# A list scheduler's overlap constants: a graph network kernel planned with less overlap between successive instructions on ScalarE, VectorE and GpSimd

## The chip, the cores and the metric

The kernel runs on one core of one Trainium2 chip. The core has five queues that run asynchronously: TensorE (PE, matrix products), ScalarE (ACT), VectorE (DVE), GpSimd (POOL) and SyncE (SP, which issues the DMAs here). Each works through its own instructions in order. The metric is the device time in microseconds (us); less is better. Where the text says "put", it means an ACT copy that empties a PSUM bank into SBUF.

## The reference

Inputs are 128 graphs of 128 nodes with 256 features, `x`, and 128 adjacency matrices, `adj`. Two layers with layer norm ahead of each are computed:

```python
# layer 0: three gated graph steps (GRU)
h = jnp.maximum(_layernorm(x, axis=-1), 0.0)
for i in range(3):
    m = jnp.einsum('bnd,de->bne', h, weight[i])
    aggr = jnp.einsum('bst,bsd->btd', A, m)          # A = (adj != 0)
    h = _gru_cell(aggr, h, w_ih, w_hh, b_ih, b_hh)
x = x + h
# layer 1: graph attention
h = jnp.maximum(_layernorm(x, axis=-1), 0.0)
Wh = h @ W;  s = Wh.sum(axis=-1)
e = jax.nn.leaky_relu(s[:, :, None] + s[:, None, :], negative_slope=0.2)
alpha = jax.nn.softmax(jnp.where(adj == 0, -jnp.inf, e), axis=-1)
x = x + alpha @ Wh
```

The GRU cell has gates r, z and n: `r` and `z` are sigmoids of sums over both inputs, `n = tanh(i_n + r * h_n)`, and `h = (1 - z) * n + z * h`.

## The kernel before

**Tiling.** The 128 graphs are taken in 32 groups of 4, so that a tile is 128 partitions by 512 columns (4 graphs of 128 nodes). A step of one group is a *turn*; there are 96 turns, and the list `turns` interleaves three groups: step 0 of group g, step 1 of group g-1, step 2 of group g-2. A turn is given 18.15 us (`SLOT`) in the plan, and it takes about 21.6 us, since other products of PE run between.

**A turn.** The state `hT` (features by nodes) is split into three bf16 parts on ACT and POOL (`turned_parts`, L609 to L616, or for rows `parts_of`, L591 and L594), turned by DMA transposes on SP (L580), and multiplied with the adjacency on PE (`edge_sums`, L634, bf16). ACT copies the sums to `aT` (L637). `node_sums` (L677 to L681) makes sums of blocks of `hT` (on POOL, `hs`) and of `aT` (on DVE, `gs`), since the weight products use a scheme with seven products in place of eight. `products` then issues the seven products for each kind, "rz" and "n", into PSUM banks `x_*`, `y_*` and `q_*`. In the first two steps of a group these are the matmuls of L708, in the last step (rows by features, `gru_rows`) those of L722.

**The put.** The bank `y_rz` is used twice in succession: product six is accumulated, `put` (L754) copies it to `t2_rz`, and product seven is accumulated on top and copied to `t3_rz`. PE runs product six of "n" between; product seven of "rz" may not start before the put of "rz" is done. DVE adds `q_rz` (L764). Gates follow on ACT (tanh, L810, L828, L834; L860 and L878 for rows) and DVE (L814 to L825, L837 to L843).

**Attention.** After step 2 of a group: layer norm (`normed`: DVE L514 and L519, POOL L523 and L524, DVE L526, ACT L530), scores, softmax (ACT exp, L1066), turned by DMA (`turned_halves_of`, ACT L1174 and L1178), PE L663 and L1099. `turned_halves` (ACT L570 and L574) turns rows by DMA likewise.

**What sets the order.** All operations are first recorded by `plan.op(engine, ns, fn, reads, writes, ...)` with a cost in ns; `Plan.run` is a list scheduler that simulates the five engines with these costs and emits the instructions in the order found. Nothing of its clock reaches the chip: only the order within each queue, and the buffers chosen along the way. The constants of the class describe the engines:

- `OVER`: by how much the next operation of an engine may start before the one ahead has ended. This is what the change edits.
- `LAG`, `SIGNAL`: what a wait across engines costs; `FLIP`: what PE loses from bf16 back to f32 matmuls; `HANDOFF`: for the port shared by DVE and POOL.

The three lines that use them are

```python
t = max(clock[e] + (self.FLIP if thin and e == "PE" and not nodes[i][8] else 0), at[i])
...
done = t + n[1]
clock[e] = done - self.OVER[e]
```

Of the operations of an engine that could start no later than the earliest possible start, the one with the smallest `rank` is taken. A rank is the latest time at which an operation must start so that the products behind it meet their due times; an operation that feeds PE's products has a further 7 us (`MARGIN`). PE's products (`due=plan.cursor`) form a chain in a fixed order; its other matmuls (edge sums, attention, transposes) are placed between by rank.

Of the kernel before, what the change touches and what calls it, by code (L numbers as in the profile page):

```python
# [41 lines left out]
class Plan:  # L42
# [5 lines left out]


    LAG = {"PE": 163, "ACT": 0, "DVE": 0, "POOL": 0, "SP": 3600}  # L50
    OVER = {"PE": 0, "ACT": 103, "DVE": 84, "POOL": 42, "SP": 0}
    FLIP, HANDOFF = 56, 120
    SIGNAL = {"PE": 53, "ACT": 36, "DVE": 36, "POOL": 78, "SP": 28}

# [62 lines left out]
    def run(self):  # L117
# [54 lines left out]
        while len(order) < len(nodes):  # L172
# [26 lines left out]
            done = t + n[1]  # L199
            clock[e] = done - self.OVER[e]  # L200
            if n[6]:
# [1013 lines left out]
```

## Time and profile before

Times of three runs: 2112.46, 2112.8 and 2113.26 us, median 2112.8. The profiled execution took 2112.71 us, its span (first to last instruction) was 2110.9 us at full TensorE clock.

| engine | busy, us | share of the span | instructions |
|---|---|---|---|
| PE (matmul) | 2084.3 | 99% | 10624 |
| PEld (weight load) | 1658.4 | 79% | 10624 |
| DVE | 1680.2 | 80% | 3626 |
| ACT | 1594.6 | 76% | 2977 |
| POOL | 921.5 | 44% | 881 |

Busy is the time in which the engine had at least one instruction running, so overlapped time counts once. A row of the waits names the waiting instruction, what it waited for, and the total in us, the number of times and the longest. A row of the timeline gives start and duration in us, the engine, the line, what is written and read, and in brackets the idle time ahead of it and what ended that.

### The profile page before, as it was taken

How to read it: one execution, taken by the hardware profiler on the slowest of the kernel's cores; microseconds unless marked ns; L12 is line 12 of the kernel's file. 1: busy time of each engine (PE TensorE's matmuls, PEld its weight loads, DVE VectorE, ACT ScalarE, POOL GpSimd, SP SyncE). 2: the span in 40 equal slices, each digit the busy share in tenths (PEclk: the TensorE clock that was granted, in tenths of full speed). 3: DMA queues.
4: the chain of work that ended last, by engine and by line, in shares of the span. 5: the costliest groups of instructions: out<-in, count | busy, mean ns of one | idle time of the engine just before them, and what ended most of it. 6: DMA issues, size and time to landing. Idle time of an engine off the chain costs nothing.

```text
span 2110.9 us, 30632 instructions
## 1 busy us (share of the span) xinstructions
PE 2084.3 (99%) x10624; PEld 1658.4 (79%) x10624; DVE 1680.2 (80%) x3626; ACT 1594.6 (76%) x2977; POOL 921.5 (44%) x881
## 2 busy tenths in 40 slices
PE   9999999999999999999999999999999999999998
PEld 7887887777877778877778777788777888788776
DVE  6678888788877887878878778887787778778777
ACT  5577877777777777777777777777778877867676
POOL 5445554334444444443355434444443444345230
PEclk9999999999999999999999999999999999999999
DMA  4322222332233223232223332232322323123321
GB/s 120 70 59 48 56 57 65 71 60 55 68 68 80 55 54 72 68 73 70 55 61 63 73 74 57 55 75 63 78 60 55 70 64 78 36 55 66 77 74 36
DMA packets 365147, 137.01 MB, mean 65 GB/s; under 512 B 296384, under 2 KB 364736, under 8 KB 364992
## 3 DMA queue, kind: packets, MB, share of 16 engines
q1 hardware_dynamic: 364992, 135.05, 29.1%
q8 instruction: 84, 1.38, 0.3%
q14 instruction: 71, 0.58, 0.1%
HBM read 45.36 MB, written 16.78 MB: 29 GB/s over the span
## 4 chain that ended last, share of the span: by engine, by line
PE 79%; ACT 10%; DVE 7%; issue 2%; DMA 0%; POOL 0%; SPq 0%; DVEq 0%; ACTq 0%; POOLq 0%
PE y_rz L708 14%; PE x_rz L708 10%; PE q_rz L708 8%; PE y_n L708 7%; PE y_rz L722 5%; PE misc L1099 5%; PE y_n L722 5%; PE misc L634 5%; PE x_n L708 4%; PE q_n L708 4%; PE q_rz L722 3%; PE x_n L722 3%; PE x_rz L722 3%; PE q_n L722 3%; ACT h L530 2%
## 5 line engine op out<-in xcount | busy, mean ns | idle before, releaser
L677 POOL TENSOR_TENSOR hs<-hT 128x512 f32<-128x512 f32 x96 | 129.5, 1350 | 304.5 <-PE y_n L722 238.9
L591 POOL TENSOR_TENSOR r<-rows 128x512 f32<-128x512 f32 x126 | 143.0, 1154 | 225.3 <-ACT rows L574 160.9
L764 DVE TENSOR_TENSOR t_rz<-t_rz,q_rz 128x512 f32<-128x512 f32 x192 | 130.8, 681 | 132.5 <-ACT t_rz L754 123.4
L754 ACT COPY t_rz<-y_rz 128x512 f32<-128x512 f32 x192 | 112.2, 584 | 146.4 <-PE y_rz L708 136.1
L708 PE MATMUL y_rz<-hs,s_hh 128*128 128x256 f32 x768 | 200.0, 383 | 1.0 <-ACT t_rz L754 0.9
L708 PE MATMUL y_rz<-gs,s_x 128*128 128x256 f32 x768 | 197.1, 379 | 0.0
L708 PEld LDWEIGHTS y_rz<-hs,s_hh 128*128 128x128 f32 x768 | 142.8, 190 | 27.1 <-ACT t_rz L754 9.2
L708 PEld LDWEIGHTS y_rz<-gs,s_x 128*128 128x128 f32 x768 | 145.9, 190 | 19.8
L594 POOL TENSOR_TENSOR p<-r 128x512 bf16<-128x512 f32 x126 | 156.9, 1264 | 0.0
L681 POOL TENSOR_TENSOR hs<-hT,hs 128x256 f32<-128x256 f32 x96 | 75.3, 785 | 177.1 <-PE q_n L722 160.7
L834 ACT ACTIVATE u<-u,bias_i 128x512 f32<-128x512 f32 x128 | 92.8, 725 | 74.0 <-DVE u L825 73.8
L764 DVE TENSOR_TENSOR t_n<-t_n,q_n 128x512 f32<-128x512 f32 x192 | 130.3, 678 | 19.9 <-ACT t_n L754 17.8
L898 POOL TENSOR_TENSOR x<-x,u 128x512 f32<-128x512 f32 x60 | 77.6, 1294 | 147.9 <-ACT u L878 62.8
L708 PE MATMUL x_rz<-hT,s_hh 128*128 128x256 f32 x512 | 131.4, 379 | 0.0
L708 PE MATMUL x_rz<-aT,s_x 128*128 128x256 f32 x512 | 131.4, 379 | 0.0
L840 DVE SCALAR_TENSOR_TENSOR d<-rz,d 128x512 f32<-128x512 f32 x128 | 117.6, 920 | 0.9
L637 ACT COPY aT<-misc 128x512 f32<-128x512 f32 x190 | 102.8, 581 | 18.1 <-PE misc L634 17.9
L616 POOL TENSOR_TENSOR pl<-d,pl 128x512 bf16<-128x512 f32 x64 | 75.7, 1183 | 89.9 <-ACT pl L614 89.8
L708 PE MATMUL y_n<-gs,s_x 128*128 128x256 f32 x384 | 114.3, 379 | 0.0
L708 PE MATMUL y_n<-hs,s_hh 128*128 128x256 f32 x384 | 114.3, 379 | 0.0
L837 DVE TENSOR_TENSOR d<-hT,u 128x512 f32<-128x512 f32 x128 | 107.3, 839 | 8.5 <-ACT u L834 6.3
L611 POOL TENSOR_TENSOR d<-hT,pl 128x512 f32<-128x512 f32 x64 | 85.6, 1339 | 63.7 <-ACT pl L609 59.0
(286 smaller groups left out, 6297.9 us busy)
## 6 DMA issues: line engine op xcount, KB each, us to landing
rows<-in_x_dram SPq DMA_DIRECT2D x32, 512.0 KB, 4.2
x<-in_x_dram SPq DMA_DIRECT2D x32, 512.0 KB, 3.9
out_dram<-x SPq DMA_DIRECT2D x31, 512.0 KB, 2.9
at<-in_adj_dram SPq DMA_DIRECT2D x32, 256.0 KB, 3.2
plT<-pl SPq DMA_TRANSPOSE x186, 3.3
peT<-pe SPq DMA_TRANSPOSE x60, 3.1
e<-in_L_gnn_weight_dram SPq DMA_DIRECT2D x3, 256.0 KB, 3.7
rz<-in_L_gnn_w_ih_dram SPq DMA_DIRECT2D x2, 384.0 KB, 4.3
```

The source lines that it names most:

```text
L591: op("POOL", 1042, lambda part=part: nc.gpsimd.tensor_tensor(ap(r1)[:, part], ap(rows)[:, part], top(rows)[:, part], OP.subtract), [(rows, ...
L594: op("POOL", 1042, lambda part=part: nc.gpsimd.tensor_tensor(ap(p3)[:, part], ap(r1)[:, part], top(r1)[:, part], OP.subtract), [(r1, n, n ...
L634: nc.tensor.matmul(flat(ps)[:, b * N:(b + 1) * N], part(i, b, k), ap(a)[:, b, :], start=(i == 0), stop=(i == 2))
L637: op("ACT", 590, lambda k=k, ps=ps: nc.scalar.copy(ap(dst)[:, k, :], flat(ps)), [ps], [(dst, 2 * k, 2 * k + 2)])
L677: op(eng, cost, lambda: sub(ap(w)[:, 0:2, :], blocks()[:, 1::2, :], blocks()[:, 0:2, :], OP.subtract), [t], [(w, 0, 2)], two=True)
L708: nc.tensor.matmul(ap(bank)[:, half, :], ap(w)[:, i - 1, gate, :], source(i, t, sums), start=(first and c == 0 and m == 0), stop=False, sk ...
L722: op("PE", 645, lambda c=c, w=w, t=t, sums=sums: nc.tensor.matmul(flat(bank)[:, c * P:(c + 3) * P], source(i, t, sums)[:, m * N:(m + 1) * ...
L754: op("ACT", 590, lambda: nc.scalar.copy(ap(t), ap(y)), [y], [t], mark=mark)
L764: op("DVE", 690, lambda: nc.vector.tensor_tensor(ap(t), ap(t), ap(q), OP.add), [q], [t])
L837: op("DVE", 690, lambda j=j, d=d, cols=cols: nc.vector.tensor_tensor(ap(d), ap(hT)[:, j, :], ap(u)[:, cols], OP.subtract), [(hT, lo, hi), ...
L840: op("DVE", 690, lambda d=d, cols=cols: nc.vector.scalar_tensor_tensor(ap(d), ap(rz)[:, 1, cols], 1.0, ap(d), op0=OP.add, op1=OP.mult), [( ...
L1099: nc.tensor.matmul(ap(ps)[:, b, :], ap(uT)[:, k, (m + b) * N:(m + b + 1) * N], ap(w1)[:, k, :], start=(k == 0), stop=(k == KD - 1))
```

## The change

Three of the five constants in `OVER` are lowered: ACT from 103 to 50, DVE from 84 to 40, and POOL from 42 to -100, which is a gap of 100 ns in place of an overlap. `PE` and `SP` stay at 0. Costs, due times, ranks' rules and the program's operations are untouched.

```diff
     LAG = {"PE": 163, "ACT": 0, "DVE": 0, "POOL": 0, "SP": 3600}
-    OVER = {"PE": 0, "ACT": 103, "DVE": 84, "POOL": 42, "SP": 0}
+    OVER = {"PE": 0, "ACT": 50, "DVE": 40, "POOL": -100, "SP": 0}
     FLIP, HANDOFF = 56, 120
```

## The prediction

> **What bounds the kernel now.** I read the page's first part, then TensorE's (PE's) own waits, then the timelines around the wait that recurs.
>
> ```profile
> PE 2084.3 (99%) x10624; PEld 1658.4 (79%) x10624; DVE 1680.2 (80%) x3626; ACT 1594.6 (76%) x2977; POOL 921.5 (44%) x881
> ```
>
> PE is idle for 2110.9 - 2084.3 = 26.6 us. Everything else on the page hides behind it, so the change can act only through these 26.6 us, through new idle time on PE, and through how PE's instructions overlap. The list of PE's waits says what the idle time is:
>
> ```profile
> PE y_rz L722 <- ACT t_rz L754: 14.1, 19, 1.3
> PE q_n L1160 <- DVE eT L1158: 1.4, 1, 1.4
> PE y_rz L708 <- ACT t_rz L754: 0.9, 2, 0.7
> ```
>
> 15.0 us are waits for one kind of ScalarE (ACT) copy, the "put" of line 754, which empties the PSUM bank y_rz before PE may accumulate into it again. PE's timeline places the others: 5.0 us in the first 30 us (seven waits, 0.16 to 1.27 us), 2.6 us from 2048 us on (five waits), and 3.8 us after PE's last matmul. The 19 waits of L722 lie between 325 and 1556 us, spaced by 64.8 us from 453 us on (453.26, 518.68, 583.45, ... 1555.67), nearly all 0.68 to 0.77 us long: the plan is periodic with three turns, and it has one stall in each period. After 1556 us the same plan has none. One such period, ACT and PE:
>
> ```profile
> 1032.24 0.72 ACT L834 ACTIVATE u<-u,bias_i 128x512 f32<-128x512 f32 x1 [1.40 <-DVE u L825]
> 1032.87 0.57 ACT L668 COPY uT<-misc 128x512 f32<-128x512 f32 x1
> 1033.34 2.08 ACT L530 ACTIVATE h<-x,nm,rs 128x256 f32<-128x256 f32 x4
> 1035.40 1.04 ACT L570 COPY pl<-hT 128x1024 uint16<-128x1024 uint16 x1
> 1036.35 0.58 ACT L754 COPY t_rz<-y_rz 128x512 f32<-128x512 f32 x1
> ```
>
> ```profile
> 1034.18 0.81 PE L722 MATMUL y_rz<-s_x,gs 128*128 128x384 f32 x2
> ...
> 1035.47 0.81 PE L722 MATMUL y_n<-s_x,gs 128*128 128x384 f32 x2
> 1036.98 0.91 PE L722 MATMUL y_rz<-s_hh,hs 128*128 128x384 f32 x2 [0.70 <-ACT t_rz L754]
> ```
>
> y_rz is complete at 1034.18 + 0.81 = 1034.99, but ACT first runs the pl copy of 1.04 us, and the put starts only at 1036.35. The put takes 0.58 us and PE resumes 0.05 us after it. Started at once, it would have released PE at 1034.99 + 0.58 + 0.05 = 1035.62, against 1036.28, the end of the y_n products: a slack of 0.66 us. The put was 1.36 us late, 1.36 - 0.66 = 0.70. So ACT's **order** costs the time, not its load. Why ACT was behind: the in-order tanh of L834 waited 1.40 us for VectorE (DVE), where
>
> ```profile
> 1030.60 1.27 DVE L679 TENSOR_TENSOR gs<-gs,aT 128x256 f32<-128x256 f32 x1
> 1031.80 0.41 DVE L825 SCALAR_TENSOR_TENSOR u<-u,t_n 128x256 f32<-128x256 f32 x1
> ```
>
> took 1.27 us for an operation that the plan prices at 0.426, while GpSimd's (POOL's) L616 ran from 1030.44 to 1031.60.
>
> In a GRU turn (L708) the slack is nil: at 1014 us the put starts at 1014.09, 0.03 us after its bank is done, runs 0.58, and the products behind it take 1.10 us instead of 1.03. ACT is mostly free there, since it waits for PE itself:
>
> ```profile
> ACT t_rz L754 <- PE y_rz L708: 136.1, 90, 2.7
> ```
>
> **What the Trainium skill says.** "ScalarE: Activation LUTs", What ACT_TABLE_LOAD costs: back-to-back ACTIVATEs overlap by about 93 ns. The trace agrees: two of 0.47 us start at 1004.05 and 1004.42, an overlap of 0.10. (DVE's L764 at 1005.35 and 1005.94 with 0.68: 0.09; POOL at 1003.49 and 1004.71 with 1.27: 0.05. The old constants 103, 84 and 42 ns are what the chip does.) "SBUF — State Buffer", SBUF: two separate sides: DVE with two SBUF inputs and POOL share a port pair as an exclusive lock, and the loser blocks. L679 above agrees. "Perfetto Trace Analysis", Identifying the Most-Contended Engine: matmul busy time is a poor measure because matmuls are pipelined. It agrees here: groups of 1.03 us start every 0.86, so I argue from the waits.
>
> **The change, part by part.** No instruction is added or removed; only the order of each queue, the buffers that go with it, and the order of DMA issues can differ. In the planner each instruction following another closely costs more: ACT 103 - 50 = 53 ns, DVE 84 - 40 = 44, POOL 42 + 100 = 142. At most that is 2977 x 0.053 = 158 us, 3626 x 0.044 = 160 and 881 x 0.142 = 125 of **planned** occupancy: ACT 76 to 83%, DVE 80 to 87%, POOL 44 to 50%. It is an upper end, since operations of several instructions count once and dependent ones are spaced by the signal cost anyway. None of it is executed.
>
> ACT, the queue that matters. From L754 y_n at 1030.25 to the put are 9 ACT instructions: 9 x 53 = 0.48 us later in the plan, plus five or so DVE steps behind u, 5 x 44 = 0.22. About 0.7 us of lateness can make the plan see the put ready before the pl copy starts, and take the put first (its rank is the earlier one). The pl copy would then go 0.6 us later, into a DMA transpose for a later turn; nothing near waits for it. This **removes** a stall: -14.1 us, at the ends 0 and -17.9 (15.0 of all put waits, and 2.9 hidden in L708, where y_rz from hs sums to 200.0 us against 197.1 from gs).
>
> The same lateness re-rolls every other put. A period has 18 puts of products (3 turns with 2 kinds and 3 puts), of which the rz ones in GRU turns have no slack. Fuller planned queues mean that more often something is running when a put comes ready: half of a 0.50 us tanh is 0.25 us, half of a 1.04 us copy 0.52, a whole copy of 1.36 (L574, L1178) the upper end. In a rows turn, 1.04 - 0.66 = 0.38 at most if ACT keeps to its plan. I take 0.30 us for one further stall of a period, and 1860 / 64.8 = 28.7 periods between 190 and 2050 us: +8.6 us. Ends: none, or two of 0.55: +31.6.
>
> DVE and POOL: nothing on PE's list in mid-run comes from them, as their chains have turns of slack; price nothing. In the fullest 20 us stretches DVE is busy for 18.9 with 36 instructions, 20.5 in the plan: there its lateness spills 0.5 us into the next stretch, where it is about 16. If that cover is gone, the tanhs behind L825 (ACT waits 73.8 us there now) delay puts, which the price above holds. SP issues the transposes (186 of plT, 3.3 us to landing) in planned order; a swap of two delays one by 3.3 us, hidden by the same turns.
>
> Switches between bf16 and f32 matmuls: x_n behind the edge sums starts its second pair 0.70 us on instead of 0.645, so 0.055 us for each of about 100 runs. Splitting or joining 20 runs is 1.1 us either way. The first 30 us and the last 60 us: 5.0 and 6.4 us of idle time; DVE is busy 9.58 of 10 us at 2080 to 2090, so another order there can cost or spare up to 3 us. I take 0 for both.
>
> **The rivals.**
> - **New put stalls, the old one kept or replaced (forecast):** for it: 18 puts, half without slack, and fuller queues in the plan than on the chip, so that the plan's order fits the chip less. The profiled execution took 2112.7 us (span 2110.9), the median is 2112.8, so nothing is to be corrected: 2112.7 + 8.6 = **2121.3 us**; own range 2117 to 2145.
> - **The stall goes and none comes (the other side):** pessimistic costs place the put ahead of the pl copy. Decides: whether the shift of 0.5 to 0.7 us exceeds the plan's lead of the pl copy over the put's release; if the chip is behind its plan by more than that, the order stays. For it: 1556 to 2040 us runs without stall; against it: there the same copy still stands ahead of the put. 2112.7 - 14.1 = 2098.6; half of it 2106.
> - **Nothing where it matters:** PE's products have a fixed order, turn buffers too, so the change does less than it says, or gains and losses cancel: 2113, within 4 us.
> - **The end alone:** put waits as now, last 60 us reordered: 2110 to 2116. It is part of the case before it.
>
> **How the numbers follow.** 0.2% (4.2 us) is about what a measurement of this kernel can tell from no change. First case 0.50, second 0.37, third 0.13. The case for a gain has one concrete place, the case for a loss has many and an open upper end; hence the order. Predicted 2121 us. Range 2097 to 2144: the second case nearly whole at its lower end, and the first up to two stalls of 0.55 us in each period. Cases of both signs hold most of it, so the likeliest one's own range stands above.
>
> **What would show it.** In the changed profile: instructions and busy times of the engines the same within 1%; PE's idle time changed by the whole difference in time. First case: PE waits on ACT L754 of more than 20 us, a good part in L708, again spaced by 65 us. Second: that row under 5 us, the put at the pl copy's place, and that copy behind it. Wrong in its base: if PE's idle time comes from DVE, POOL or DMA in mid-run, or if PE's busy time moves by more than 5 us.

## The result, and the profile after

The changed kernel takes 2087.57 us (median of 4 runs, 2087.14 to 2088.78) against 2113.03 for the kernel before: a ratio of 0.9879, with a 95% interval of 0.9861 to 0.9896. It is **faster by 1.2%**, 25 us. The forecast was slower, 2121 us, with a range of 2097 to 2144: the sign was wrong, and the result lies 9 us below the range.

The span fell from 2110.9 to 2086.0 us. The page's first part, then all of TensorE's (PE's) waits; the columns are total us, times, longest:

```profile
PE 2076.1 (100%) x10624; PEld 1663.5 (80%) x10624; DVE 1664.8 (80%) x3626; ACT 1598.8 (77%) x2977; POOL 932.8 (45%) x881
```

```profile
PE misc L452 <- DMA e<-in_L_gnn_weight_dram: 1.6, 1, 1.6
PE misc L363 <- DMA rz<-in_L_gnn_w_ih_dram: 1.5, 1, 1.5
PE y_rz L326 <- DVE zeros L324: 1.2, 1, 1.2
PE misc L649 <- ACT hT L547: 0.7, 1, 0.7
PE x_rz L1160 <- DVE eT L1158: 0.6, 1, 0.6
PE q_rz L1156 <- ACT s_all L1066: 0.3, 1, 0.3
```

Four of the six belong to the first 22 us, two to the last 10. Between 22 and 2076 us the profile shows no wait of PE: both rows of waits on the put (ScalarE's, ACT's, line 754) are gone. The reader is to see in the first line that the instructions are as many as before, and that PE's *busy* time fell too, by 8.2 us. Nothing of PE's work became shorter. The rest of this document rests on that remark, so it is worked out here.

A pair of L722 matmuls is shown as 0.81 us long, but pairs start every 0.645 us, each before the shown end of the last. Idle time in the profile begins only at that end. So a wait costs more than its idle time: in the period shown before, PE started at 1035.47 and then at 1036.98, and 1.51 - 0.645 = 0.87 us are lost, of which 0.70 is shown as idle and the rest as busy. Taken over all of PE's instructions (time from each start to the next, less the median for that kind of matmul) the trace of before has some 32 us lost, that of after some 7; the level depends on what is counted as one kind. That the two differ by about the 24.9 us of the spans follows from the count itself, since both traces hold the same matmuls. What the count adds is where the loss lies: the 19 waits of L722 are 17.2 us of it. The remaining 7.7 us of the gain are scattered: 2.0 from the slow start of the pair after each of these waits, some 1.5 from two or three waits of L708, 1.8 after the last L722 product (the wait of q_n, L1160, for eT, 1.4 us, is gone), 0.65 ahead of the first, and the rest in small pieces.

The place that stalled once in each period, in the changed kernel; ACT, then PE:

```profile
1019.10 1.05 ACT L570 COPY pl<-hT 128x1024 uint16<-128x1024 uint16 x1
1020.04 0.59 ACT L668 COPY uT<-misc 128x512 f32<-128x512 f32 x1
1022.15 0.58 ACT L754 COPY t_rz<-y_rz 128x512 f32<-128x512 f32 x1 [1.51 <-PE y_rz L722]
```

```profile
1021.24 0.81 PE L722 MATMUL y_rz<-s_x,gs 128*128 128x384 f32 x2
1021.89 0.81 PE L722 MATMUL y_n<-s_hh,hs 128*128 128x384 f32 x2
1022.53 0.81 PE L722 MATMUL y_n<-s_x,gs 128*128 128x384 f32 x2
1023.18 0.81 PE L722 MATMUL y_rz<-s_hh,hs 128*128 128x384 f32 x2
```

Here a pl copy still stands **ahead** of the put, but ACT has done it and is waiting: it now waits 1.51 us for PE, where it had been 1.36 us late. The put starts 0.10 us after its bank is complete (1021.24 + 0.81 = 1022.05), and PE runs on at its step of 0.645. In its order this place is not typical. `plan.run` returns the numbers of the operations, which are the same in both kernels; by these numbers 23 pl copies stood directly ahead of such a put in the kernel before, and in the changed one 16 of the 23 come behind that put, 3 some places ahead, and 4 directly ahead (there the eight matmuls of L1099 stand between on PE, so that it needs the bank later). That ACT now waits for PE holds more widely. The first row is of the kernel before, the second of the changed one:

```profile
ACT t_rz L754 <- PE y_rz L722: 9.9, 12, 2.1
```

```profile
ACT t_rz L754 <- PE y_rz L722: 46.3, 39, 2.4
```

### The profile page after: what moved, and what is told of

Same layout as the page of the kernel before. It is cut to its first block, busy times and chain, and to the rows that moved or that the text cites. A ratio compares the mean times of both kernels' runs of the same rounds, so it can differ in the third digit from the quotient of the medians.

```text
span 2086.0 us, 30762 instructions
## 1 busy us (share of the span) xinstructions
PE 2076.1 (100%) x10624; PEld 1663.5 (80%) x10624; DVE 1664.8 (80%) x3626; ACT 1598.8 (77%) x2977; POOL 932.8 (45%) x881
## 4 chain that ended last, share of the span: by engine, by line
PE 99%; DMA 0%; DVE 0%; ACT 0%; SPq 0%; issue 0%; DVEq 0%; ACTq 0%
PE y_rz L708 16%; PE q_rz L708 11%; PE x_rz L708 11%; PE y_n L708 8%; PE misc L634 6%; PE y_n L722 6%; PE y_rz L722 6%; PE x_n L708 5%; PE q_n L708 5%; PE misc L1099 5%; PE q_n L722 4%; PE x_n L722 4%; PE q_rz L722 4%; PE x_rz L722 4%; PE misc L663 3%; PE misc L463 1%
## 5 line engine op out<-in xcount | busy, mean ns | idle before, releaser
L591 POOL TENSOR_TENSOR r<-rows 128x512 f32<-128x512 f32 x126 | 149.2, 1203 | 317.1 <-ACT rows L574 170.5
L677 POOL TENSOR_TENSOR hs<-hT 128x512 f32<-128x512 f32 x96 | 128.2, 1335 | 196.7 <-PE y_n L722 83.4
L754 ACT COPY t_rz<-y_rz 128x512 f32<-128x512 f32 x192 | 112.1, 584 | 125.7 <-PE y_rz L708 78.4
L708 PE MATMUL y_rz<-hs,s_hh 128*128 128x256 f32 x768 | 198.9, 382 | 0.0
L708 PE MATMUL y_rz<-gs,s_x 128*128 128x256 f32 x768 | 197.2, 379 | 0.0
L708 PEld LDWEIGHTS y_rz<-hs,s_hh 128*128 128x128 f32 x768 | 144.0, 190 | 23.4 <-ACT t_rz L754 4.7
L708 PEld LDWEIGHTS y_rz<-gs,s_x 128*128 128x128 f32 x768 | 146.2, 190 | 19.6
L708 PE MATMUL x_rz<-hT,s_hh 128*128 128x256 f32 x512 | 131.4, 379 | 0.0
L708 PE MATMUL x_rz<-aT,s_x 128*128 128x256 f32 x512 | 131.4, 379 | 0.0
L611 POOL TENSOR_TENSOR d<-hT,pl 128x512 f32<-128x512 f32 x64 | 79.7, 1247 | 90.5 <-ACT pl L609 44.7
L708 PE MATMUL y_n<-hs,s_hh 128*128 128x256 f32 x384 | 114.4, 380 | 0.0
L708 PE MATMUL y_n<-gs,s_x 128*128 128x256 f32 x384 | 114.3, 380 | 0.0
L1099 PE MATMUL misc<-w,uT 128*128 128x256 f32 x480 | 112.8, 379 | 0.0
L708 PEld LDWEIGHTS x_rz<-hT,s_hh 128*128 128x128 f32 x512 | 97.4, 190 | 19.2
L708 PEld LDWEIGHTS x_rz<-aT,s_x 128*128 128x128 f32 x512 | 97.4, 190 | 13.0
L677 DVE TENSOR_TENSOR gs<-aT 128x512 f32<-128x512 f32 x96 | 78.2, 814 | 36.7 <-ACT aT L637 35.3
```

What stands on the lines that cost most here:

```text
L591: op("POOL", 1042, lambda part=part: nc.gpsimd.tensor_tensor(ap(r1)[:, part], ap(rows)[:, part], top(rows)[:, part], OP.subtract), [(rows, ...
L611: op("POOL", 1158, lambda k=k, r=r: nc.gpsimd.tensor_tensor(ap(r), ap(hT)[:, k], part(pl, k, 0), OP.subtract), [(hT, 2 * k, 2 * k + 2), (p ...
L677: op(eng, cost, lambda: sub(ap(w)[:, 0:2, :], blocks()[:, 1::2, :], blocks()[:, 0:2, :], OP.subtract), [t], [(w, 0, 2)], two=True)
L708: nc.tensor.matmul(ap(bank)[:, half, :], ap(w)[:, i - 1, gate, :], source(i, t, sums), start=(first and c == 0 and m == 0), stop=False, sk ...
L754: op("ACT", 590, lambda: nc.scalar.copy(ap(t), ap(y)), [y], [t], mark=mark)
L1099: nc.tensor.matmul(ap(ps)[:, b, :], ap(uT)[:, k, (m + b) * N:(m + b + 1) * N], ap(w1)[:, k, :], start=(k == 0), stop=(k == KD - 1))
```

## The experiments

All times are medians. The kernel before gave 2111.6 to 2112.9 us beside them. mild_optim and handoff105 were timed twice, pool_plus and pess_a three times, the others four to twelve times. "Tight" puts are those of y_rz in a rows turn whose bank PE needs again within 2.2 us of its completion.

| run | edit to the kernel before | us | ratio, 95% interval | PE waits on L754 |
|---|---|---|---|---|
| act_only | ACT 50 | 2094.5 | 0.9913, 0.9899 to 0.9928 | 2.0 us |
| dve_only | DVE 40 | 2092.4 | 0.9909, 0.9893 to 0.9926 | 0.2 |
| act_dve | ACT 50, DVE 40 | 2093.7 | 0.9914, 0.9899 to 0.9928 | 3.1 |
| half | ACT 76, DVE 62 | 2093.4 | 0.9911, 0.9895 to 0.9928 | 1.5 |
| pess_a | ACT 90, DVE 73 | 2096.8 | 0.9931, 0.9908 to 0.9953 | 1.6 |
| more | ACT 0, DVE 0, POOL -100 | 2093.7 | 0.9913, 0.9897 to 0.9930 | 0.5 |
| pool_only | POOL -100 | 2118.4 | 1.0029, 1.0017 to 1.0041 | 19.7, nearly all in L708 |
| pool_plus | POOL 184 | 2098.0 | 0.9938, 0.9916 to 0.9961 | 3.6 |
| mild_optim | ACT 120, DVE 96 | 2127.8 | 1.0080, 1.0051 to 1.0110 | 21.3, mostly in L708 |
| optim | ACT 150, DVE 120 | 2134.9 | 1.0111, 1.0096 to 1.0126 | 27.9, mostly in L708 |
| handoff | HANDOFF 135 | 2095.0 | 0.9919, 0.9904 to 0.9933 | 2.7 |
| handoff105 | HANDOFF 105 | 2094.2 | 0.9921, 0.9893 to 0.9950 | 1.3 |
| margin8 | MARGIN 8000 | 2114.3 | 1.0010, 1.0001 to 1.0018 | 15.0, mostly in L722 |
| put_first | 23 swaps in ACT's queue | 2094.5 | 0.9918, 0.9903 to 0.9932 | 1.8 |

### Is it the place of the put in ACT's queue?

put_first keeps the plan of the kernel before and edits its order afterwards (an excerpt, with comments added; `puts` and `longs` are filled where the operations are recorded):

```diff
+    def put_first(order):
+        for i in puts:                       # puts of y_rz after product six, rows turns
+            at = order.index(i)
+            j = max(p for p in range(at) if plan.nodes[order[p]][0] == "ACT")
+            if order[j] in longs:            # the pl copies of L570
+                order.insert(at, order.pop(j))
+        return order
...
-        for i in plan.run():
+        for i in put_first(plan.run()):
```

> The kernel before with its own plan; afterwards, at 23 places of ScalarE's queue, the put of y_rz is set ahead of the pl copy (L570) that stood directly before it. All other queues are the same instruction for instruction. Theory A (the order of put and pl copy is what costs): the 18 of 19 L722 waits that stand behind such a copy go. From start to start a wait costs 1036.98 - 1035.47 - 0.645 = 0.87 us, more than the 0.70 shown as idle, so 18 x 0.87 = 15.7 us: 2097 us, PE waits on ACT L754 under 3 us. Theory B (ScalarE is short of time there and the order is a symptom): the stall moves to the next put or to the work behind the pl copy; 2108 to 2115 us.

It gave 2094.5 us. Its ACT timeline, same place:

```profile
1023.52 0.72 ACT L834 ACTIVATE u<-u,bias_i 128x512 f32<-128x512 f32 x1 [1.40 <-DVE u L825]
1024.15 0.57 ACT L668 COPY uT<-misc 128x512 f32<-128x512 f32 x1
1024.61 2.08 ACT L530 ACTIVATE h<-x,nm,rs 128x256 f32<-128x256 f32 x4
1026.59 0.56 ACT L754 COPY t_rz<-y_rz 128x512 f32<-128x512 f32 x1
1027.06 1.04 ACT L570 COPY pl<-hT 128x1024 uint16<-128x1024 uint16 x1
```

ACT is as late as before (the same 1.40 us wait for u), and the pl copy and all behind it come after the put; nothing is lost by that. So Theory A, as it is put here, holds, and Theory B falls: 23 exchanged instructions on one engine, with every other queue the same, are worth 18.4 us, three quarters of the whole gain. 18 waits of 0.87 account for 15.7 of them; after each wait the next pair had also started 0.75 instead of 0.645 us on, which is 1.9 more.

### Which of the three constants?

Here and below, the lines of several runs stand in one fence.

```diff
-    OVER = {"PE": 0, "ACT": 103, "DVE": 84, "POOL": 42, "SP": 0}
+    OVER = {"PE": 0, "ACT": 50, "DVE": 84, "POOL": 42, "SP": 0}     # act_only
+    OVER = {"PE": 0, "ACT": 103, "DVE": 40, "POOL": 42, "SP": 0}    # dve_only
+    OVER = {"PE": 0, "ACT": 103, "DVE": 84, "POOL": -100, "SP": 0}  # pool_only
```

> The constant for ScalarE alone is lowered (103 to 50). Theory A (a plan with slower ScalarE takes the put first): most of the gain, 2088 to 2098 us, the pl copy behind the put in rows turns. Theory C (any other order re-rolls the stalls, and the constants mean nothing in particular): a time anywhere from 2085 to 2125 us.

> The constant for VectorE alone is lowered (84 to 40). Theory A, if ScalarE's lateness comes from VectorE (tanh waiting 1.4 us for u ahead of the stall): a good part of the gain, 2090 to 2105 us. If ScalarE's own cost is what counts: 2108 to 2116. Theory C: anywhere from 2085 to 2125 us.

> The constant for GpSimd alone is lowered (42 to -100). Theory A (ScalarE and VectorE planned slower): no gain, 2108 to 2118 us. Theory D (the gap on GpSimd lets VectorE take the shared port between two GpSimd operations, in the plan, and the VectorE chain ahead of the tanh comes right): most of the gain, 2088 to 2100 us. Theory C: anywhere from 2085 to 2125 us.

ACT alone gives 18.4 us, DVE alone 20.5 us. Neither is needed beside the other, so the effects don't add: each removes the same stall. GpSimd (POOL) alone costs 5.5 us: the stall of the rows turns goes there too, but PE now waits in the GRU turns,

```profile
PE y_rz L708 <- ACT t_rz L754: 18.7, 20, 2.4
```

which is what my forecast had said of the whole change. Next, both without POOL, and more of everything:

```diff
+    OVER = {"PE": 0, "ACT": 50, "DVE": 40, "POOL": 42, "SP": 0}     # act_dve
+    OVER = {"PE": 0, "ACT": 0, "DVE": 0, "POOL": -100, "SP": 0}     # more
```

> ScalarE 50 and VectorE 40 as in the changed kernel, GpSimd left at 42. Theory A (planned lateness of ScalarE and VectorE puts the copies in a safer order; GpSimd matters little beside them): 2085 to 2093 us, no row of PE waits on L754 over 3 us. Theory C (each set of constants is a new draw): as likely between 2093 and 2120.

> ScalarE and VectorE at 0 (no overlap at all), GpSimd at -100. Theory A: as the changed kernel or a little better, 2084 to 2093 us, since PE's waits are already gone and nothing is left to win but about 6 us at the ends. If too much caution costs (planned queues of over 90% push work late): 2095 us and more. Theory C: anywhere from 2085 to 2125 us.

Both come to 2093.7, each 0.7 us above what Theory A had allowed, act_dve with three waits of L708, 3.1 us in all. "more" is no better and no worse than act_dve, so further caution did nothing here. POOL at -100 costs 5.5 us by itself, and on top of ACT 50 and DVE 40 (act_dve against the changed kernel) it is worth some 6 us: it has no sign of its own.

### Does the direction matter, or is any new order as good?

```diff
+    OVER = {"PE": 0, "ACT": 150, "DVE": 120, "POOL": 42, "SP": 0}   # optim
+    OVER = {"PE": 0, "ACT": 76, "DVE": 62, "POOL": 42, "SP": 0}     # half
-    FLIP, HANDOFF = 56, 120
+    FLIP, HANDOFF = 56, 135                                         # handoff
-MARGIN = 7000
+MARGIN = 8000                                                       # margin8
```

> The other direction: ScalarE 150 and VectorE 120, more overlap than the trace shows; GpSimd 42. Theory A (what counts is that the plan is not faster than the chip): slower than the kernel before or equal to it, 2112 to 2145 us, with PE waits on ACT L754 of 15 us and more. Theory C: as likely faster, 2085 to 2112.

> About half of the step on ScalarE and VectorE (76 and 62), GpSimd left at 42. Theory A (a plan that is slower than the chip on these two engines takes puts first, one that is faster doesn't): between the kernel before and the full step, 2092 to 2108 us; at the lower end if the stall goes at once when the put comes ready ahead of the pl copy. Theory C (each set of constants is a new draw): anywhere from 2085 to 2135.

> A change of another constant, as a measure of what a new draw of the order does by itself: HANDOFF 135 in place of 120, so that the shared port comes free 15 ns earlier in the plan; the overlap constants stay as before. 2207 of the lines of ScalarE's order differ from the kernel before, against 4917 for the change. Theory A: the stall of the rows turns stays or moves, 2105 to 2120 us. Theory C: anywhere from 2085 to 2135.

> Another new draw: MARGIN 8000 in place of 7000, so that everything that feeds a product is ranked 1 us earlier; the overlap constants stay as before. Theory A: a rank doesn't help where the put isn't ready in the plan when ScalarE takes the pl copy, so the stall stays, 2106 to 2118 us. Theory E (it is urgency, not lateness, that was missing): 2090 to 2100. Theory C: anywhere from 2085 to 2135.

More overlap than the trace shows is 23 us slower, with the waits in the GRU turns; half of the step gives as much as the whole step of act_dve. But handoff, which plans nothing slower, gave 2095.0, and Theory A had said 2105 or more. Its ACT timeline shows how:

```profile
1023.26 0.59 ACT L668 COPY uT<-misc 128x512 f32<-128x512 f32 x1 [1.28 <-PE misc L663]
1023.74 2.07 ACT L530 ACTIVATE h<-x,nm,rs 128x256 f32<-128x256 f32 x4
1025.72 1.03 ACT L570 COPY pl<-hT 128x1024 uint16<-128x1024 uint16 x1
1026.79 0.59 ACT L754 COPY t_rz<-y_rz 128x512 f32<-128x512 f32 x1
```

By kind this is the order of the kernel before, h, pl, put. But the tanh of L834 had its u in time, so ACT waits for PE (L663) and not for VectorE (DVE), and the put starts 0.09 us after its bank is done, though the pl copy is directly ahead of it. Counted in the traces over the tight puts: before, 21 stand behind h and pl and start 1.06 us late on average; in handoff 23 stand behind the same two, and start 0.09 us late; in put_first 23 stand behind h and start 0.28 us late; in the changed kernel the 26 tight puts have eleven different pairs ahead of them, none more than five times, and start 0.09 us late on average, 0.22 at most. So two things had to meet: a long copy planned directly ahead of the put, and ACT arriving late there because DVE was late. put_first takes away the first, handoff the second, and either removes the stall; a third shows in pess_a, below. margin8 moved few instructions (a line diff of ACT's order in the two traces has 274 lines, against 1648 for the change), kept both, and kept the stall; so urgency (Theory E) was not what was missing.

Four more orders, three without the change's direction:

```diff
+    OVER = {"PE": 0, "ACT": 120, "DVE": 96, "POOL": 42, "SP": 0}    # mild_optim
+    FLIP, HANDOFF = 56, 105                                         # handoff105
+    OVER = {"PE": 0, "ACT": 103, "DVE": 84, "POOL": 184, "SP": 0}   # pool_plus
+    OVER = {"PE": 0, "ACT": 90, "DVE": 73, "POOL": 42, "SP": 0}     # pess_a
```

> A little more overlap than the trace shows: ScalarE 120, VectorE 96, GpSimd 42. Theory A (the direction decides): 2108 us or more, PE waits on ACT L754 of 10 us or more. Theory F (a wait arises where a long copy stands ahead of a put and ScalarE comes late to it; the kernel before is an unlucky order, and any new one may be free of it): below 2100 us about as often as for less overlap.

> HANDOFF 105 in place of 120 (135 gave 2095 us), overlap constants as before: a new draw with about 80% as many lines of ScalarE's order changed as in the changed kernel. Theory A: 2105 to 2120 us. Theory F: below 2100 as likely as not.

> GpSimd's constant moved as far the other way (42 to 184), ScalarE and VectorE as before. Theory A: 2105 to 2122 us, with waits on L754 of 10 us or more. Theory F: below 2100 as likely as not.

> A small step the way of the change: ScalarE 90, VectorE 73, GpSimd 42. Theory A: 2088 to 2108 us. Theory F: 2088 to 2100 or above 2105 with equal chances.

Three of these four are free of the stall in every period, two of them without planning ACT or DVE slower; mild_optim has new ones in the GRU turns. pess_a is free of the old one in a way that the two conditions above don't cover. ACT, then PE:

```profile
1022.69 0.72 ACT L834 ACTIVATE u<-u,bias_i 128x512 f32<-128x512 f32 x1 [1.40 <-DVE u L825]
1025.87 1.04 ACT L570 COPY pl<-hT 128x1024 uint16<-128x1024 uint16 x1
1026.83 0.58 ACT L754 COPY t_rz<-y_rz 128x512 f32<-128x512 f32 x1
```

```profile
1024.61 0.81 PE L722 MATMUL y_rz<-s_x,gs 128*128 128x384 f32 x2
1025.90 0.81 PE L722 MATMUL y_n<-s_x,gs 128*128 128x384 f32 x2
1026.54 1.89 PE L1099 MATMUL misc<-w,uT 128*128 128x256 f32 x8
1028.27 0.81 PE L722 MATMUL y_rz<-s_hh,hs 128*128 128x384 f32 x2
```

ACT waits the same 1.40 us for u, runs the same copies in the same order, and the put is 1.41 us late; no time is lost. What differs is PE's order: the eight attention matmuls of L1099 stand ahead of product seven of "rz". In the kernel before they come behind it:

```profile
1037.73 0.81 PE L722 MATMUL y_rz<-s_x,gs 128*128 128x384 f32 x2
1038.38 1.89 PE L1099 MATMUL misc<-w,uT 128*128 128x256 f32 x8
```

With them between, PE needs the bank 2.85 us after its completion; without them and without a stall (handoff) it needs it after 1.13. 19 places of pess_a are like this, with the pl copy directly ahead of a put that is 1.41 us late on average, and none of them stalls. half and pool_plus have these matmuls there too, in 22 and 21 places. So **three things had to meet**: a long copy directly ahead of the put, ACT late because DVE was late, and nothing but product six of "n" between on PE. put_first, handoff and pess_a each take away one of them; put_first does so with no other change, handoff and pess_a are other plans as a whole, read from their traces.

So for the size of the gain Theory F is right, though its condition was short of one term: the kernel before was an unlucky order. Of the 14 other plans (the changed kernel among them) only margin8 keeps the stall of every period; three (pool_only, mild_optim, optim) have waits in the GRU turns instead, and ten have neither (at most three single waits for a put each). Of the five that leave the constants of ACT and DVE alone, three (handoff, handoff105, pool_plus) are 14 to 17 us faster and two (pool_only, margin8) are not. The direction seems to add safety: all seven plans with less overlap on ACT or DVE are at 2097 us or below, and both with more are at 2128 and above, the larger step slower. Theory A, that the direction decides, is right for ACT and DVE as a tendency, with only two plans on the one side, and wrong as a condition. Why caution is safe is not shown. That an order found with slower engines is reached early on the chip would be one reason; pess_a, where ACT is as late as before, speaks against it as the only one.

### What does a late put cost?

Two kernels keep the changed kernel's plan and order and make the put last longer, by repeating the same copy (set on several lines here, with comments added):

```diff
-  op("ACT", 590, lambda: nc.scalar.copy(ap(t), ap(y)), [y], [t], mark=mark)
+  op("ACT", 590, lambda: [nc.scalar.copy(ap(t), ap(y)) for _ in range(
+      3 if rows and t.tag == "t2_rz" else 1)], [y], [t], mark=mark)      # rows_x3
+      2 if not rows and t.tag == "t2_rz" else 1)], [y], [t], mark=mark)  # gru_x2
```

> The changed kernel with its own plan and order; the put of y_rz after product six in the last step of each group (32 times) makes its copy three times over, the same copy to the same place, so that its result comes about 2 x 0.48 = 0.95 us later. In 24 of the 32 places PE runs only the two pairs of y_n between. If the slack there is the 0.66 us of the prediction: 24 x 0.29 = 7 us, 2094.5. If it is 0.40 us, as start times after the put's end give (0.45 less the 0.05 of a release): 24 x 0.55 = 13 us, 2101. If lateness of a put doesn't reach PE: 2088.

> The changed kernel with its own plan and order; in the first two steps of each group the put of y_rz after product six makes its copy twice, the same copy to the same place, and so ends 0.618 us later (the spacing of such copies where they were made three times). By the trace 22 of these places have a slack of 0.02 us, and the next have 0.8. If the slack is what the trace gives: 22 x (0.618 - 0.024) = 13.1 us, 2100.7 us. If PE's queue hides part of it: 2088 to 2097.

rows_x3 took 2110.3 us, 9 more than the higher expectation and 22.7 more than the changed kernel; its profiled execution was the fastest of twelve, 2108.3. ACT, then PE, in its trace:

```profile
1029.17 1.82 ACT L754 COPY t_rz<-y_rz 128x512 f32<-128x512 f32 x3 [1.51 <-PE y_rz L722]
```

```profile
1029.56 0.81 PE L722 MATMUL y_n<-s_x,gs 128*128 128x384 f32 x2
1031.04 0.91 PE L722 MATMUL y_rz<-s_hh,hs 128*128 128x384 f32 x2 [0.68 <-ACT t_rz L754]
```

The expectation had the price of the copies wrong, not the higher slack that it named: the repeated copies start 0.618 us apart, without any overlap (each waits for a semaphore that the one ahead raises at its end), so the put ended 2 x 0.618 = 1.24 us later. PE lost 1.48 - 0.645 = 0.84 us, and 1.24 - 0.84 = **0.40 us is the slack** in a rows turn, not 0.66. 24 places of 0.84 are 20.2 us (the trace has 25 such waits, 20.5 us from start to start); the spans differ by 2106.5 - 2086.0 = 20.5. gru_x2, priced with the measured spacing, took 2101.6 us, 14.0 more than the changed kernel, where 13.1 were expected: in 22 places of the GRU turns there is no slack. Its row shows only 10.3 us of idle time, since part of each wait again passes as busy:

```profile
PE y_rz L708 <- ACT t_rz L754: 10.3, 22, 1.3
```

## Why the prediction was wrong

**The place was right.** The 19 waits of L722 were the largest part of what PE lost, and 18 of them hung on the pl copy ahead of the put, as put_first shows. The chain behind it was right as far as u: in handoff, with u in time, ACT's order of h, pl and put has no stall. I had set DVE's block on the port that it shares with GpSimd (the Trainium skill, "SBUF — State Buffer", SBUF: two separate sides) at the head of the chain, and this is not shown. In handoff DVE's operations are stretched as well (L825 takes 1.27 us there, 0.41 in the kernel before), but DVE takes L825 ahead of the sums of L677 and L679:

```profile
1018.50 1.27 DVE L825 SCALAR_TENSOR_TENSOR u<-u,t_n 128x256 f32<-128x256 f32 x1
1021.01 1.65 DVE L677 TENSOR_TENSOR gs<-aT 128x512 f32<-128x512 f32 x1
```

So u's place in DVE's queue can be the reason as well as the block.

**The step that failed is the "re-roll" of the other puts.** I priced it at +8.6 us, one new wait of 0.30 us in each period, and gave the case for a gain 0.37. The changed kernel has not one wait of PE for a put, so this term was 0, and the old stall, which the forecast kept, went. Orders like that exist: pool_only, mild_optim and optim have just those waits in the GRU turns, 18.7 to 24.8 us of idle time. But none of the seven plans with less overlap on ACT or DVE has more than 3.1 us of them. What I had left out is that the stalled order itself was the exception. The view that says so was on my table: the trace of before had nothing of the kind from 1556 us on, and I set it against the gain because there the copy still stood ahead of the put. It spoke for it: at 1618, 1682 and 1746 us the put starts 0.09 us after its bank is done, with the copy directly ahead. ACT was on time there, so the stall hangs on little. The forecast also looked for the effect of a new order mainly in ACT's queue; that PE's own other matmuls move, and that this can end the stall (pess_a), was in no term of it but the 1.1 us for switches.

**The mechanism of the gain was right in part.** In the case for a gain I had the put move ahead of the pl copy. That is worth 18 us where it is done by hand, and in the changed kernel it happened at 16 of 23 places. But ACT comes in time as well, and half, pess_a, handoff, handoff105 and pool_plus still have a pl copy directly ahead of 22 or 23 of these puts and are without the stall. So the condition I named (the shift exceeding the plan's lead of the copy) was one of three ways out, and not needed.

**The size of the gain was too small**, and so the lower end of the range. 14.1 us was the idle time of the waits. Measured from start to start they are 17.2, with the slow start after each 19. The ends, which I set at 0, gave about 2.5 (0.65 and 1.8), and waits and small delays in L708 the rest. My own end of -17.9 had tried to cover what is hidden behind the modelled ends, but only for L708.

**The slack of a rows turn** was 0.40 us, not 0.66, for the same reason: it was taken to the shown end of a matmul, not to the start that the next one would have had. In the GRU turns it was nil, as stated.

**The signs.** The instructions stayed the same, as said, and the busy times within 1%, but for GpSimd's (921.5 to 932.8 us, 1.2%). PE's idle time was to change by the whole difference in time; it fell from 26.6 to 9.9 us, by 16.7 of the 24.9. The rest is PE's busy time, which moved by 8.2 us, and I had named this as a mark that the base was wrong. It was: not that PE's idle time came from elsewhere, but that idle and busy are no clean division on this engine. The sentence of the Trainium skill that I cited ("Perfetto Trace Analysis", Identifying the Most-Contended Engine) says that busy time is a poor measure because matmuls are pipelined; I applied it to the busy time and not to the idle time that is left over.

**What stays open:** why the changed kernel is 6 us better than act_dve. act_dve's PE has three L708 waits (3.1 us in all) and two single waits on DVE (1.1 and 0.8 us) that the changed kernel lacks; pool_only shows that the same constant can as well cost 5.5 us. I take it for luck of the draw, and no run tells more.

## What to carry to other kernels

A list scheduler's order is one draw among many; where the profile shows one short stall in every period of an otherwise full engine, ask first which other order would be free of it. If a part of the same run already is, expect that many changes of the costs remove it, and give a gain the larger chance: here 13 of 14 did, though three of them brought other stalls. Plan engines a little slower than they are rather than faster: in this kernel 13% to 100% less overlap on ACT or DVE cost nothing, and 15% more cost 16 us. Measure stalls of TensorE from start to start. And count all places of a kind before you say what an order has ahead of what; one place of the timeline can be the exception.

## What the runs showed of the hardware

- Successive copies of ScalarE overlap by 0.10 us (0.585 us long, 0.48 apart). The repeated copies of rows_x3 don't: 64 pairs start 0.595 to 0.621 us apart. Their records name the reason: each waits for a semaphore that ScalarE's own copy ahead raises, and starts 0.03 us after that copy's end. This is a wait that the program holds; whether the engine would overlap them without it is not shown.
- PE needs 0.05 us from the end of a put to the next product, and the put starts 0.04 (L708) to 0.09 us (L722) after the shown end of the product that completes its bank.
- After a wait the next pair of L722 starts 0.75 us on instead of 0.645 (1036.98 to 1037.73), so each wait costs 0.1 us beyond itself (2.0 us over the 19 waits of the kernel before, 2.6 over the 25 of rows_x3).
